# A node's own product in a graph layer: from additions on GpSimd during the sort to a trip through DRAM and additions on VectorE

## The chip, the cores and the metric

The kernel runs on one core of one Trainium2 chip. Its time is the device time of one execution in microseconds; the lower, the better. Of each kernel one execution is also recorded by the hardware profiler, and what is quoted as a view (the page, the timeline, the waits, the chain) is that one execution.

## What is computed

A network of two layers works on 6250 nodes of 256 float32 features. 100,000 edges (src, dst, weight) come sorted by dst. Layer 0's graph step sums over the edges towards their **src** node, so the edges have to be sorted anew; layer 1's sums towards their dst, in the order that is given.

```python
def _L0_gnn_ref(x, edge_row, edge_col, edge_val, weight_l, bias_l, weight_r, bias_r):
    h = x @ weight_l
    msgs = edge_val[:, None] * h[edge_col]
    agg = jax.ops.segment_sum(msgs, edge_row, num_segments=N)
    out = agg + bias_l
    out = out + x @ weight_r + bias_r        # x @ weight_r: the node's own product
    return out

x = x + _L0_gnn_ref(_layernorm(x), src, dst, edge_weight, ...)
x = x + _L0_ffn_ref(_layernorm(x), ...)      # 8 experts, softmax gates, three matmuls each
x = x + _L1_gnn_ref(_layernorm(x), src, dst, edge_weight, ...)
x = x + _L1_ffn_ref(_layernorm(x), ...)      # 32 experts, the best one for each node
```

## The kernel before, in words

The nodes stand in 49 tiles of 128, one node to a partition, and stay in SBUF for the whole kernel as `X` (128 x 49 x 256, float32). The work has three stages.

**The sort** (about the first 390 us) runs over 25 groups of 4096 edges. In each group VectorE builds one-hot patterns and ranks from them (`hot`, `same`, `picked`, `pos`), payloads (`loads`, line 527) and a one-hot of target places (`to`, line 523); TensorE counts (lines 464 to 474) and then moves the payloads to their places with 32 matmuls into `put` (line 530); ScalarE copies counts (`start`, `total`), multiplies the last payload (line 502) and takes the result out (`there`, line 533); GpSimd adds the pieces of the result into the table `Z` (lines 535 to 539) and notes sizes (line 489). `settle_group` updates running counts on VectorE in small instructions (lines 482, 484, 486, 488).

In between, each group also makes layer 0's products for two of the node tiles (`center0`, `products0`): the layer norm's statistics on VectorE (line 547), the centred rows on ScalarE (line 556), two transposes (line 340), four matmul passes that make both products at once (`ph`, line 570; the left half of the result is h, the right half the node's own product), and a copy with the factor of the norm into `hs` (line 571). GpSimd then adds the own product and the bias to `X` (lines 572 and 573), and SyncE's queue stores h in DRAM as `h0` (line 574).

**Layer 0** (about 390 to 1830 us). Its 15 blocks have 1, 1, 2, 3, then nine times 4, and 3 and 3 tiles. For a block, `edges0` reads the sorted edges out of `Z` on VectorE (lines 671 to 686) into an index list `idx`, of which three are kept. The generator `aggregate0` then goes over tiles and over 18 columns of 128 edges each: GpSimd gathers 128 rows of `h0` by an indirect DMA (line 201) into one of 12 buffers `g`, ScalarE and VectorE multiply by the edge weights (`m`, lines 230 and 231; six buffers), VectorE makes one-hots for three columns at a time (`s`, line 222), and TensorE accumulates in `acc` (line 701). After a tile's last column VectorE adds both halves of `acc` to `X` (line 704). The dense experts of an earlier block stand between these steps on TensorE (lines 748 and 760); how many columns come before each dense step is planned by `aheads`. VectorE adds each expert's result from PSUM to `X` (line 762). `end0` normalises the block and stores it as `h1` by SyncE's queue (lines 771 and 773). The first 64 columns of layer 1 already run here, with their own copies of indices and weights, `idx_e` and `w_e` (lines 806 to 812).

**Layer 1** (from about 1830 us) does the like with `h1`, in the edge order that is given.

Within an engine, instructions run in the order in which the built program has them. That order is made by a scheduler, which may move an instruction ahead of others of its engine where the data allow it; the diff alone doesn't show it.

Of the kernel before, what the change touches and what calls it, by code (L numbers as in the profile page):

```python
# [8 lines left out]
F32 = mybir.dt.float32  # L9
F32R = mybir.dt.float32r  # L10
BF = mybir.dt.bfloat16
I32 = mybir.dt.int32
AF = mybir.ActivationFunctionType
OP = mybir.AluOpType
AX = mybir.AxisListType

P = 128
N = 6250
D = 256
E = 100000  # L20
NT = 49
NLAST = N - (NT - 1) * P
NB = 4
EW = 18
# [25 lines left out]
def gnn_ffn_kernel(ctx: ExitStack, tc: tile.TileContext, a, out):  # L50
# [29 lines left out]

    nc = tc.nc

    const = ctx.enter_context(tc.tile_pool(name="const", bufs=1))
    dram = ctx.enter_context(tc.tile_pool(name="dram", bufs=1, space=bass.MemoryType.DRAM))
    work = ctx.enter_context(tc.tile_pool(name="work", bufs=2))

    X = const.tile([P, NT, D], F32, name="X")
    h0 = dram.tile([NT * P, D], F32, name="h0")  # L90
    h1 = dram.tile([NT * P, D], F32, name="h1")

    def across(name, pool=const):

        row = a[name]
        t = pool.tile([P, row.shape[0]], F32, name=name + "_b")
        nc.scalar.dma_start(t, bass.AP(tensor=row.tensor, offset=row.offset, ap=[[0, P], [1, row.shape[0]]]))
        return t
# [9 lines left out]
    src_c = const.tile([P, NCOL], I32, name="src_c")  # L108
    val_c = const.tile([P, NCOL], F32, name="val_c")
# [24 lines left out]
    early = sort_ctx.enter_context(tc.tile_pool(name="early", bufs=1))  # L134
    psum = sort_ctx.enter_context(tc.tile_pool(name="psum0", bufs=1, space=bass.MemoryType.PSUM))
# [51 lines left out]
    wlr = early.tile([P, 2, 2, D], F32, name="wlr")  # L187
    nc.scalar.dma_start(wlr[:, :, 0, :], a["L0_gnn_weight_l"].rearrange("(k p) d -> p k d", p=P))
    nc.scalar.dma_start(wlr[:, :, 1, :], a["L0_gnn_weight_r"].rearrange("(k p) d -> p k d", p=P))
    bias0 = across("L0_gnn_bias_l", early)  # L190
    bias0r = across("L0_gnn_bias_r", early)
    nc.gpsimd.tensor_add(bias0, bias0, bias0r)
    bias1 = across("L1_gnn_bias")
# [5 lines left out]
    def gather(pool, h, idx, ahead):  # L199
        g = pool.tile([P, D], F32, tag="g", name="g", bufs=ahead)  # L200
        nc.gpsimd.indirect_dma_start(out=g, out_offset=None, in_=h,  # L201
                                     in_offset=bass.IndirectOffsetOnAxis(ap=idx, axis=0))
        return g
# [14 lines left out]
    def one_hots(pool, dl, j, hots):  # L218

        s = pool.tile([P, SJ, P], F32R, tag="s", name="s", bufs=hots)  # L220
        n = min(SJ, dl.shape[1] - j)
        nc.vector.tensor_tensor(s[:, :n], col[:, None, :].to_broadcast([P, n, P]),  # L222
                                dl[:, j:j + n, None].to_broadcast([P, n, P]), OP.is_equal)
        return s

    def weighted(pool, h, idx, w, ahead, parts):

        g = gather(pool, h, idx, ahead)
        m = pool.tile([P, 2, D], F32R, tag="m", name="m", bufs=parts)
        nc.scalar.activation(m[:, 0, :], g, AF.Copy, scale=w)  # L230
        nc.vector.scalar_tensor_tensor(m[:, 1, :], g, w, m[:, 0, :], op0=OP.mult, op1=OP.subtract)  # L231
        return m
# [3 lines left out]
    def columns1(pool, psum, js, h, idx, w, bufs):  # L236


        hots, ahead, parts, few = bufs
        first = js.start == 0  # L240
        ends = []

        def summed(q, acc):

            yield
            if first and (q % 2 or q == 2 * NB):
                s = first_sums[:, q // 2, :]
            else:
                s = pool.tile([P, D], F32, tag="sums", name="sums", bufs=few)
            nc.scalar.activation(s, acc[:, 0, :], AF.Copy)  # L250
            nc.vector.tensor_add(s, s, acc[:, 1, :])
            halves[q] = s
            low, high = slice(0, P // 2), slice(P // 2, P)
            if q % 2:
                nc.vector.tensor_add(s[low], s[low], halves[q - 1][low])
            elif first:
                if 0 < q < 2 * NB:
                    nc.vector.tensor_add(halves[q - 1][high], halves[q - 1][high], s[high])
            else:
                if q == 2 * NB:  # L260
                    nc.vector.tensor_add(s, s, first_sums[:, NB, :])
                nc.vector.tensor_add(halves[q - 1][high], halves[q - 1][high], s[high])
                sT = pool.tile([P, 2, P], F32, tag="sT", name="sT", bufs=2)
                yield
                yield from by_weight(psum, halves[q - 1], sT, q // 2 - 1)

        for j in range(js.start, js.stop + (0 if first else LAG)):
            if j < js.stop:
                q, i = divmod(j + CS // 2, CS)
                opens = i == 0 or j == js.start  # L270
                done = i == CS - 1 or j == js.stop - 1
                if opens:
                    acc = psum.tile([P, 2, D], F32, tag="agg", name="acc", bufs=2)
                if (j - js.start) % SJ == 0:
                    s = one_hots(pool, dl_c, j, hots)
                m = weighted(pool, h, idx[:, j:j + 1], w[:, j:j + 1], ahead, parts)
                nc.tensor.matmul(acc, s[:, (j - js.start) % SJ, :], m, start=opens, stop=done)  # L277
                if done:
                    ends.append((j, summed(q, acc)))
            for at, steps in ends:  # L280
                if j - at in (0, 2, LAG - 4, LAG - 1):
                    next(steps, None)
            yield
        for _, steps in ends:
            for _ in steps:
                pass
        yield
# [271 lines left out]
    def products0(tiles, xn, std):  # L559

        n = len(tiles)
        rstd = work.tile([P, NB], F32, tag="rstd0", name="rstd0")
        nc.vector.reciprocal(rstd[:, :n], std[:, :n])
        hs = early.tile([P, 2, 2, D], F32, tag="hs", name="hs", bufs=2)
        for j, t in enumerate(tiles):
            nT = early.tile([P, 2, P], F32, tag="nT", name="nT", bufs=2)
            transposed(psum, xn[:, j, :], nT)
            ph = psum.tile([P, 2, D], F32, tag="mm", name="ph", bufs=2)
            for k in range(2):
                nc.tensor.matmul(ph, nT[:, k, :], wlr[:, k], start=(k == 0), stop=(k == 1))  # L570
            nc.scalar.activation(hs[:, j], ph, AF.Copy, scale=rstd[:, j:j + 1])
            nc.gpsimd.tensor_add(X[:, t, :], X[:, t, :], hs[:, j, 1, :])
            nc.gpsimd.tensor_add(X[:, t, :], X[:, t, :], bias0)
        nc.sync.dma_start(h0[tiles[0] * P:(tiles[0] + n) * P, :].rearrange("(t p) d -> p t d", p=P), hs[:, :n, 0, :])


    pairs = [[t for t in (2 * g, 2 * g + 1) if t < NT] for g in range(NG)]
# [41 lines left out]
    psum = dense_ctx.enter_context(tc.tile_pool(name="psum1", bufs=1, space=bass.MemoryType.PSUM))  # L619
# [12 lines left out]
    LIM = late[0] * P  # L632
    NE = EARLY * GC

    with tc.tile_pool(name="layer0", bufs=1) as wp, tc.tile_pool(name="outs0", bufs=1, side="right") as wo_pool, \
# [56 lines left out]
        def aggregate0():  # L692
            for b, tiles in enumerate(blocks0):
                idx, dl, w = edges[b]
                for i, t in enumerate(tiles):
                    acc = psum.tile([P, 2, D], F32, tag="agg", name="acc", bufs=2)
                    for j in range(EW):
                        if j % SJ == 0:
                            s = one_hots(wp, dl[:, i, :], j, 3)
                        m = weighted(wp, h0, idx[:, i, j:j + 1], w[:, i, j:j + 1], 12, 6)  # L700
                        nc.tensor.matmul(acc, s[:, j % SJ, :], m, start=(j == 0), stop=(j == EW - 1))  # L701
                        if j == EW - 1:
                            for half in range(2):
                                nc.vector.tensor_add(X[:, t, :], X[:, t, :], acc[:, half, :])
                        yield

            for _ in columns1(wp, psum, range(NE), h1[:LIM, :], idx_e, w_e, (3, 12, 6, 2)):
                yield
            while True:
                yield  # L710
# [84 lines left out]
        def load1(k, half):  # L795
# [4 lines left out]
            else:  # L800
                cs = slice(half * NC1 // 2, (half + 1) * NC1 // 2)
                x = a["L1_ffn_W2"].rearrange("e h d -> (e h) d").rearrange("(c p) d -> p c d", p=P)
                nc.sync.dma_start(w2f[:, cs, :], x[:, cs, :])


        idx_e = wp.tile([P, NE], I32, name="idx_e")
        w_e = wp.tile([P, NE], F32, name="w_e")

        def early_columns():
            nc.vector.tensor_scalar(w_e, src_c[:, :NE], float(LIM), None, op0=OP.is_lt)  # L810
            nc.vector.tensor_tensor(w_e, w_e, val_c[:, :NE], OP.mult)
            nc.vector.tensor_scalar(idx_e, src_c[:, :NE], float(LIM - 1), None, op0=OP.min)


        n_late = len(late)
# [67 lines left out]
        sums = Stream(aggregate0())  # L883
# [41 lines left out]
        hs = end0(late)  # L925
# [14 lines left out]
    with tc.tile_pool(name="layer1", bufs=1, reuse_waits="tile") as wp, \  # L940
# [74 lines left out]
        with tc.tile_pool(name="flow1", bufs=1, reuse_waits="tile") as flow:  # L1015

            sums = Stream(columns1(flow, psum, range(NE, NREAL), h1, src_c, val_c, (5, EW + 6, 12, 4)))
# [5 lines left out]
            for ins in done:  # L1023
                behind.enter_context(tc.issue_after(ins.ins))
            nc.vector.tensor_scalar(sel_x, which_x[:, :, None].to_broadcast([P, NX1, H1]), 0.0, FAR,
                                    op0=OP.is_equal, op1=OP.mult)
            nc.vector.memset(nought, 0.0)
            hm = hidden1(flow, block, 0)
            for b, tiles in enumerate(blocks1):
                n = len(tiles)  # L1030
# [79 lines left out]
```

## Time and profile before

| | us |
|---|---|
| three runs | 2892.92, 2898.83, 2900.43; median 2898.83 |
| the profiled execution | 2895.13, with a span of 2893.4 |
| TensorE busy in the span | 2677.7 (93%) |
| VectorE busy | 2012.4 (70%) |
| ScalarE busy | 1626.1 (56%) |
| GpSimd busy | 1926.1 (67%) |
| mean granted TensorE clock | 0.974 |

The span is the time from the first to the last recorded instruction; 1.7 us of the profiled execution lie around it. Busy shares are means over stages with different limits, so each stage has to be read by itself. GpSimd's gathers, x882 in layer 0, take 1.024 us each (line 201). GpSimd's additions of line 572 take 1.585 us in the mean and those of line 573 1.067 us, 48 of each within the first 375 us.

### The profile page before, as it was taken

Reading aid. Unit: us, or ns where it says so; the run is one execution under the profiler, and the core shown is the slowest. Engines: PE = TensorE matmul, PEld = TensorE weight load, DVE = VectorE, ACT = ScalarE, POOL = GpSimd, SP = SyncE. Lnnn points to the kernel's source line nnn. Section 1 sums busy time; section 2 is a strip of 40 time slices with the busy share of each in tenths; the row PEclk is TensorE's granted clock in tenths of the full one; section 3 lists DMA queues with packets and bytes.
Section 4 is the critical chain, followed back from the end, with each engine's and each line's share of the span. In section 5 each row is a group of like instructions: output and inputs, shape, how many; then the busy total and the mean of one; then the engine's idle time right before and its main releaser. Section 6 shows DMA issues by size and latency. Waiting matters only on the chain.

```text
span 2893.4 us, 37030 instructions
## 1 busy us (share of the span) xinstructions
PE 2677.7 (93%) x10336; PEld 1750.2 (60%) x10336; DVE 2012.4 (70%) x4917; ACT 1626.1 (56%) x3790; POOL 1926.1 (67%) x1932
## 2 busy tenths in 40 slices
PE   5888848888999999999999998779999999999998
PEld 2444427665566666666666665556666666666666
DVE  8999977778768767766566555666666666666630
ACT  6777737655555555555555545455555555555532
POOL 4666667777767676766675527677777777777720
PEclk9999978999999999999999999999999999999999
DMA  4000043333333333333332214333333333333310
GB/s 150 19 19 19 19 141 97 101 100 102 92 99 95 90 101 97 91 100 96 91 102 82 78 39 135 109 108 103 107 108 109 106 108 102 108 106 109 109 44 12
DMA packets 123140, 260.73 MB, mean 90 GB/s; under 512 B 32236, under 2 KB 68904, under 8 KB 122920
## 3 DMA queue, kind: packets, MB, share of 16 engines
q0 software_dynamic: 79872, 218.21, 26.2%
q1 hardware_dynamic: 31672, 32.42, 3.4%
q10 hardware_dynamic: 11376, 7.60, 0.8%
q8 instruction: 85, 1.39, 0.2%
q14 instruction: 135, 1.11, 0.1%
HBM read 238.87 MB, written 19.25 MB: 89 GB/s over the span
## 4 chain that ended last, share of the span: by engine, by line
PE 65%; DVE 17%; DMA 8%; issue 4%; ACT 4%; POOL 1%; ACTq 0%; POOLq 0%; DVEq 0%
PE ph L748 19%; PE py L760 10%; PE py L1000 9%; PE ph L984 9%; PE acc L701 6%; PE acc L277 4%; DMA g<-h,src_c 4%; DMA g<-h,idx 3%; DVE loads L527 3%; DVE to L523 2%; DVE m L231 2%; ACT m L230 2%; PE ph L987 1%; PE ph L214 1%; POOL g L201 1%
## 5 line engine op out<-in xcount | busy, mean ns | idle before, releaser
L201 POOL DMA_INDIRECT g<-h,idx x882 | 903.1, 1024 | 391.8 <-DVE m L231 175.2
L201 POOL DMA_INDIRECT g<-h,src_c x718 | 725.6, 1011 | 227.8 <-issue 104.2
L230 ACT ACTIVATE m<-g,w 128x256 fp32r<-128x256 f32 x882 | 394.7, 500 | 260.0 <-PE acc L701 136.0
L751 ACT ACTIVATE hT<-ph,shift,scale 128x512 f32<-128x512 f32 (+3 forms) x480 | 329.0, 696 | 314.6 <-PE ph L748 313.4
L230 ACT ACTIVATE m<-g,val_c 128x256 fp32r<-128x256 f32 x718 | 349.7, 503 | 273.6 <-PE acc L277 132.2
L231 DVE SCALAR_TENSOR_TENSOR m<-g,val_c,m 128x256 fp32r<-128x256 f32 x718 | 337.1, 483 | 211.2 <-ACT m L230 207.6
L231 DVE SCALAR_TENSOR_TENSOR m<-g,w,m 128x256 fp32r<-128x256 f32 x882 | 397.7, 476 | 42.5 <-ACT m L230 41.4
L748 PE MATMUL ph<-nT,w 128*128 128x512 f32 (+3 forms) x960 | 373.1, 524 | 25.0 <-ACT hT L751 24.8
L760 PE MATMUL py<-wo,hT 128*128 128x256 f32 x1568 | 382.1, 387 | 13.8 <-DVE X L762 10.5
L1000 PE MATMUL py<-w,hm 128*128 128x256 f32 x1568 | 386.7, 385 | 3.1 <-ACT hm L989 3.1
L701 PE MATMUL acc<-m,s 128*128 128x512 f32 x882 | 341.4, 490 | 38.0 <-DVE scale L657 24.7
L984 PE MATMUL ph<-nT,w 128*128 128x512 f32 (+2 forms) x832 | 374.8, 571 | 0.0
L748 PE MATMUL ph<-hT,w 128*128 128x512 f32 (+3 forms) x960 | 368.5, 518 | 0.5 <-ACT hT L751 0.5
L760 PEld LDWEIGHTS py<-wo,hT 128*128 128x128 f32 x1568 | 294.7, 193 | 80.8 <-DVE X L762 26.9
L277 PE MATMUL acc<-m,s 128*128 128x512 f32 x782 | 332.2, 499 | 1.7 <-DVE m L231 1.7
L1000 PEld LDWEIGHTS py<-w,hm 128*128 128x128 f32 x1568 | 292.1, 193 | 52.9 <-ACT hm L989 4.6
L222 DVE TENSOR_TENSOR s<-col,dl 128x384 fp32r<-128x384 f32 x294 | 161.4, 551 | 187.0 <-PE acc L701 184.8
L748 PEld LDWEIGHTS ph<-nT,w 128*128 128x128 f32 x960 | 175.2, 195 | 174.2 <-issue 118.1
L989 ACT ACTIVATE hm<-ph,b 128x512 f32<-128x512 f32 (+2 forms) x208 | 136.8, 659 | 200.0 <-PE ph L987 199.6
L748 PEld LDWEIGHTS ph<-hT,w 128*128 128x128 f32 x960 | 176.2, 193 | 118.9 <-issue 88.3
L701 PEld LDWEIGHTS acc<-m,s 128*128 128x128 f32 x882 | 169.7, 195 | 109.8 <-issue 48.9
L984 PEld LDWEIGHTS ph<-nT,w 128*128 128x128 f32 x832 | 157.2, 191 | 101.5 <-issue 81.1
(248 smaller groups left out, 3359.0 us busy)
## 6 DMA issues: line engine op xcount, KB each, us to landing
g<-h,idx POOLq DMA_INDIRECT x882, 2.8
g<-h,src_c POOLq DMA_INDIRECT x718, 2.8
h<-hs SPq DMA_DIRECT2D x25, 256.0 KB, 2.1
X<-in_x_dram SPq DMA_DIRECT2D x12, 512.0 KB, 8.9
out_dram<-o SPq DMA_DIRECT2D x11, 512.0 KB, 3.4
h<-hs SPq DMA_DIRECT2D x9, 512.0 KB, 3.0
w<-in_L_ffn_W_dram ACTq DMA_DIRECT2D x2, 2048.0 KB, 11.2
wo<-in_L_ffn_Wo_dram ACTq DMA_DIRECT2D x1, 2048.0 KB, 20.0
```

What stands on the lines that cost most here:

```text
L201: nc.gpsimd.indirect_dma_start(out=g, out_offset=None, in_=h, in_offset=bass.IndirectOffsetOnAxis(ap=idx, axis=0))
L222: nc.vector.tensor_tensor(s[:, :n], col[:, None, :].to_broadcast([P, n, P]), dl[:, j:j + n, None].to_broadcast([P, n, P]), OP.is_equal)
L230: nc.scalar.activation(m[:, 0, :], g, AF.Copy, scale=w)
L231: nc.vector.scalar_tensor_tensor(m[:, 1, :], g, w, m[:, 0, :], op0=OP.mult, op1=OP.subtract)
L277: nc.tensor.matmul(acc, s[:, (j - js.start) % SJ, :], m, start=opens, stop=done)
L701: nc.tensor.matmul(acc, s[:, j % SJ, :], m, start=(j == 0), stop=(j == EW - 1))
L748: nc.tensor.matmul(ph[:, :nw], (w1, w2)[layer][:, e, k, m * P:(m + 1) * P], src[:, k, :nw], start=(k == 0), stop=(k == 1))
L751: nc.scalar.activation(hT[:, m, :nw], ph[:, :nw], AF.Relu, bias=shift[:, layer, c:c + 1], scale=scale[:, layer, c:c + 1])
L760: nc.tensor.matmul(py, hT[:, k, j * P:(j + 1) * P], wo[:, e, k, :], start=(k == 0), stop=(k == 1))
L984: nc.tensor.matmul(ph[:, :nw], w1f[:, k, c * P:(c + 1) * P], nT[:, k, :nw], start=(k == 0), stop=False)
L989: nc.scalar.activation(hm[:, :nw], ph[:, :nw], AF.Relu, bias=b1[:, c:c + 1])
L1000: nc.tensor.matmul(py[:, j, :], now[:, cols], w2f[:, c, :], start=False, stop=(c == NC1 - 1), skip_group_check=True)
```

## The change

The sort no longer adds anything to `X`. `products0` stores both halves of `hs`: h in `h0`, as before, and the own product in a second DRAM tensor, `own0`. In layer 0, `aggregate0` loads the own product of each tile from `own0` into one of two buffers (`own`, by SyncE's queue) and lets VectorE add first the bias and then the own product to `X`; in the source these two additions stand before the tenth of a tile's 18 columns. The bias row stays in SBUF for the whole kernel, and for that and for the `own` buffers the gathers of layer 0 have 11 buffers instead of 12. The early columns of layer 1 use `src_c` and `val_c`, which are altered in place, and `idx_e` and `w_e` are gone, with one VectorE instruction fewer.

```diff
+    own0 = dram.tile([NT * P, D], F32, name="own0")
...
-    bias0 = across("L0_gnn_bias_l", early)
+    bias0 = across("L0_gnn_bias_l")
...
             nc.scalar.activation(hs[:, j], ph, AF.Copy, scale=rstd[:, j:j + 1])
-            nc.gpsimd.tensor_add(X[:, t, :], X[:, t, :], hs[:, j, 1, :])
-            nc.gpsimd.tensor_add(X[:, t, :], X[:, t, :], bias0)
-        nc.sync.dma_start(h0[tiles[0] * P:(tiles[0] + n) * P, :].rearrange("(t p) d -> p t d", p=P), hs[:, :n, 0, :])
+        for i, h in enumerate((h0, own0)):
+            nc.sync.dma_start(h[tiles[0] * P:(tiles[0] + n) * P, :].rearrange("(t p) d -> p t d", p=P), hs[:, :n, i, :])
...
                 for i, t in enumerate(tiles):
+                    own = wp.tile([P, D], F32, tag="sums", name="own", bufs=2)
+                    nc.sync.dma_start(own, own0[t * P:(t + 1) * P, :])
                     acc = psum.tile([P, 2, D], F32, tag="agg", name="acc", bufs=2)
                     for j in range(EW):
+                        if j == EW // 2:
+                            nc.vector.tensor_add(X[:, t, :], X[:, t, :], bias0)
+                            nc.vector.tensor_add(X[:, t, :], X[:, t, :], own)
                         if j % SJ == 0:
                             s = one_hots(wp, dl[:, i, :], j, 3)
-                        m = weighted(wp, h0, idx[:, i, j:j + 1], w[:, i, j:j + 1], 12, 6)
+                        m = weighted(wp, h0, idx[:, i, j:j + 1], w[:, i, j:j + 1], 11, 6)
...
-            for _ in columns1(wp, psum, range(NE), h1[:LIM, :], idx_e, w_e, (3, 12, 6, 2)):
+            for _ in columns1(wp, psum, range(NE), h1[:LIM, :], src_c, val_c, (3, 11, 6, 2)):
...
-        idx_e = wp.tile([P, NE], I32, name="idx_e")
-        w_e = wp.tile([P, NE], F32, name="w_e")
         def early_columns():
-            nc.vector.tensor_scalar(w_e, src_c[:, :NE], float(LIM), None, op0=OP.is_lt)
-            nc.vector.tensor_tensor(w_e, w_e, val_c[:, :NE], OP.mult)
-            nc.vector.tensor_scalar(idx_e, src_c[:, :NE], float(LIM - 1), None, op0=OP.min)
+            nc.vector.scalar_tensor_tensor(val_c[:, :NE], src_c[:, :NE], float(LIM), val_c[:, :NE],
+                                           op0=OP.is_lt, op1=OP.mult)
+            nc.vector.tensor_scalar(src_c[:, :NE], src_c[:, :NE], float(LIM - 1), None, op0=OP.min)
```

## The prediction, made before the changed kernel was run

> **What bounds the kernel now.** I read the busy time of the engines by stretches first, since the page's shares are means over stages. Columns: stretch, its length, then PE, PEld, DVE, ACT and POOL busy (instructions), granted clock, DMA share, GB/s.
>
> ```profile
> 200.00:250.00 50.00, 43.60 (x199) 22.43 (x198) 49.98 (x109) 38.19 (x142) 30.94 (x34) 1.00 0.05 17
> ...
> 500.00:600.00 100.00, 82.23 (x358) 67.12 (x358) 72.78 (x181) 62.87 (x137) 77.00 (x75) 0.91 0.37 101
> ...
> 800.00:1000.00 200.00, 199.82 (x692) 126.03 (x692) 146.37 (x368) 113.70 (x216) 139.83 (x139) 1.00 0.34 97
> ```
>
> Three limits. In the sort VectorE never rests (49.98 of 50). From 800 us to about 1700 TensorE never rests. Between them GpSimd issues gathers without a break: 75 in 100 us at 1.03 us each, with 0.30 us between two, which leaves nothing of the 100. That ramp is paced by the gathers.
>
> Next, VectorE's timeline in the sort: start, duration, line. The first four rows are a usual group (at 254 us), the last four come from groups where no addition on GpSimd lay beside the instruction.
>
> ```profile
> 254.11 0.75 DVE L482 SCALAR_TENSOR_TENSOR ZJ<-base_of,part,full_of 128x49 bf16<-128x49 bf16 x1
> ...
> 254.75 0.73 DVE L484 TENSOR_SCALAR wrap<-total 128x49 f32<-128x49 f32 x1
> ...
> 255.58 0.67 DVE L486 TENSOR_TENSOR base_of<-total,wrap 128x49 bf16<-128x49 f32 x1
> ...
> 257.13 0.88 DVE L497 TENSOR_TENSOR same<-tq 128x256 bf16<-128x256 bf16 x1
> ...
> 35.09 0.20 DVE L486 TENSOR_TENSOR base_of<-total,wrap 128x49 bf16<-128x49 f32 x1
> ...
> 36.16 0.40 DVE L497 TENSOR_TENSOR same<-tq 128x256 bf16<-128x256 bf16 x1
> ...
> 46.89 0.40 DVE L482 SCALAR_TENSOR_TENSOR ZJ<-base_of,part,full_of 128x49 bf16<-128x49 bf16 x1
> ...
> 47.72 0.18 DVE L484 TENSOR_SCALAR wrap<-total 128x49 f32<-128x49 f32 x1
> ```
>
> Four small instructions take 0.75 + 0.73 + 0.67 + 0.88 = 3.03 us where 1.18 would do. GpSimd's timeline has its four additions exactly there:
>
> ```profile
> 251.99 2.63 POOL L572 TENSOR_TENSOR X<-X,hs 128x256 f32<-128x256 f32 x1 [0.53 <-ACT hs L571]
> 254.70 0.73 POOL L573 TENSOR_TENSOR X<-X,L_gnn_bias_l_b 128x256 f32<-128x256 f32 x1
> 255.39 0.79 POOL L572 TENSOR_TENSOR X<-X,hs 128x256 f32<-128x256 f32 x1
> 256.26 1.47 POOL L573 TENSOR_TENSOR X<-X,L_gnn_bias_l_b 128x256 f32<-128x256 f32 x1
> ```
>
> So VectorE loses 1.85 us in each group of 14.30 to them. That looks like 40 us over the sort. The decisive question is who waits for VectorE. The start of `put` on TensorE, with the idle time before it in brackets:
>
> ```profile
> 96.92 0.84 PE L530 MATMUL put<-loads,to 128*128 128x245 bf16 x3
> ...
> 111.18 0.83 PE L530 MATMUL put<-loads,to 128*128 128x245 bf16 x3
> ...
> 125.42 0.84 PE L530 MATMUL put<-loads,to 128*128 128x245 bf16 x3
> ...
> 381.61 7.40 PE L530 MATMUL put<-loads,to 128*128 128x245 bf16 x32 [3.04 <-DVE to L523]
> ```
>
> While VectorE still had some lead, TensorE went round in 14.26 and 14.24 us. Its loop has its own waits, all on ScalarE after TensorE's own results (0.88 us for `start`, 0.88 for `nT`, seen in every group). VectorE goes round in 14.30. Freed of 1.85 us, VectorE would be ready early and TensorE's loop would bind at 14.24.
>
> [...]of the gathers of layer 1, the 165 that lie beside VectorE's additions of two SBUF tiles exceed the shortest (0.94) by 0.087 us in the mean, and so do the others. [...]line 776, the same kind, took 411 here, and 0.34 from one start to the next. [...]the store of `h0` landed in 2.1.
>
> **The change part by part.**
>
> *98 additions leave GpSimd.* First group: `over` (0.73 against 0.18 to 0.27) and `to` (2.52 against 2.27) stand beside line 572 and 573, and `put` waits 2.71 us for `to`: 0.75 us gained. Fourth group: `put` waits 0.70 for a `to` of 2.75: 0.70. From 139.66 to 368.42, 16 rounds in 228.76 us, 14.297 each; 14.24 instead: 0.9. Last group: `put` waits 3.04, VectorE being behind; it would be up to 4.5 us ahead, held back only by `total`: 3.0. Sum **-5.4 us**. The rest of the 40 us becomes idle time of VectorE.
>
> *25 more stores of 256 KB on SyncE's queue.* DMA is 5 to 7% busy there, `hs` has two buffers of 28 us; the load for `check_edges` stands one store later, needed 15 us after. Nothing.
>
> *The start of layer 0.* The built program's order moves the additions far forward: on VectorE six bias and six own additions stand before the first `m`. 12 x 0.34 = 4.1 us; but the small work of `missing` and `early_columns`, and about 2.4 us of a later block's `edges0`, leave the same place. I count the first `m` 0.6 us earlier, and the first index list 0.15 earlier. The first own load is issued when the sort has ended, and its addition comes some 2.8 us later: against 2.1 us of landing it may wait, 0 to 1 us; I take +0.3.
>
> *The ramp, up to gather 270 (770 us).* 19 own and 19 bias additions fall there, 13 us of VectorE. They are hidden: VectorE itself stands still for 8.2 us at the end of the ramp, because a new `idx` has to wait for gather 270, eight gathers beyond its own `m`:
>
> ```profile
> 770.05 0.20 DVE L682 TENSOR_SCALAR idx<-bothi 128x72 int32<-128x72 int32 x1 [8.24 <-DMA g<-h,idx]
> ...
> 772.82 3.78 PE L760 MATMUL py<-wo,hT 128*128 128x256 f32 x8 [3.88 <-DVE X L762]
> ```
>
> In the new order it stands at the same `m`, so the pace stays the gathers'. If each addition holds up a gather by 0 to 0.14 us, that costs 0 to 5; from the 165 gathers I take 0.03: +1.2. Eleven buffers suffice: the lead of gathers over `m` I count in the ramp is at most about 7, and in the 8 us stop the queue gets just 11 ahead.
>
> *The stretch that TensorE binds.* The remaining 24 own and 24 bias additions (16 us) crowd in the next 110 us or so. Cover: line 222 waits 30.1 us for TensorE between 760 and 1000. But own loads have two buffers, so each starts when the addition two before is done and lands 2.1 us or more later; in places three stand close together, and VectorE then waits, some 5 us in all, with evictions (line 762) behind it. I take +0.8, 0 to 4. SyncE's stores of `h1` stand behind own loads whose buffers are by then free; nobody waits for them. After it, layer 0's tail and layer 1 are as before: nothing.
>
> Sum: -5.4 + 0.3 + 1.2 + 0.8 = **-3.1 us** on the profiled 2895.1, whose span is 2893.4. The median of the runs is 3.7 above that execution, so: 2898.8 - 3.1 = 2895.7.
>
> **The rivals.**
> *VectorE's relief passes on* (faster). If TensorE's loop shortens with VectorE, because ScalarE's order was waiting for it after all, 22 groups x 1.85 = 41 us: 2858; a third of it gives 2885. For it: VectorE is 100% busy and the chain of waits runs through it. Against: TensorE's rounds of 14.24 with VectorE ahead, and ScalarE's idle 2.9 us per group, all on `put`.
> *The own loads stall VectorE* (slower). 18 of them come while the count of `m` stands between 307 and 334. Two buffers and 2.1 us make about 19 us of waiting, plus 13 us of additions, in a stretch of some 38 us; TensorE's evictions have two PSUM buffers. It decides when waits and additions there exceed what line 222 waits anyway; with half uncovered, +15 - 3 = 2911.
> *The change isn't what the source says*: that holds already, since the additions run ahead of their columns instead of in the midst; it only moves costs between ramp and later stretch.
>
> **How the numbers follow.** A difference under 0.3% (8.7 us) is about what a measurement of this kernel can tell from no change. The likeliest case, 0.6, has its own range 2890 to 2901. The faster rival, with orders of the new program that happen to fit better, 0.24; the slower one 0.16. Within the likeliest a few hundredths pass the bound on the fast side. Faster 0.3, same 0.53, slower 0.17. The range reaches from a fifth of the faster rival to two thirds of the slower: 2882 to 2908.
>
> **What would show it.** Right: lines 482, 484, 486, 497 back near 1.2 us together, VectorE with idle time in the sort, `put` every 14.24 us, its last wait gone, the stage's end some 5 us earlier; gathers still back to back to about 765; TensorE full from 800 to 1700. Wrong: rounds of `put` well under 14.2, long waits on `own` loads on VectorE with TensorE idle behind, or gathers above 1.1 us.

## The result, and the profile after

The changed kernel takes **2911.85 us** (median of six runs, 2905.60 to 2916.97) against 2898.81 of the kernel before in the same session: a ratio of 1.0045, 95% interval 1.0030 to 1.0061. It is slower by 13 us; the prediction had 3 us faster, with 2908 as its upper end. The profiled execution took 2907.63, with a span of 2905.8 (before: 2893.4).

On the chips of the first seven experiments (no_adds, no_load, eleven, pinned, no_adds_again, adds_in_sort, late_in_sort) the kernel before took 3229 to 3282 us. There the product that reads a gather started late: in no_adds 10.3 us after the gather's end (median of the first 264), where it was 2.8 in the kernel before. Why is not known. So of these seven I read the sort and the durations of instructions, and their ratios carry little.

In the changed kernel, lines 482 to 571 of the sort stand two lower (484 to 573), and line 201 is now 203, 231 is 233, 682 is 683, 701 is 708, 762 is 769. First the busy time by stretches, with the columns of the same view before (length; PE, PEld, DVE, ACT, POOL; clock, DMA share, GB/s):

```profile
200.00:250.00 50.00, 42.92 (x191) 22.11 (x190) 45.33 (x114) 40.64 (x152) 23.15 (x24) 1.00 0.10 32
500.00:600.00 100.00, 78.25 (x342) 61.36 (x343) 70.36 (x184) 61.85 (x134) 77.61 (x74) 0.95 0.37 101
800.00:1000.00 200.00, 196.87 (x679) 123.32 (x678) 161.76 (x420) 111.40 (x211) 143.44 (x134) 0.99 0.37 106
```

VectorE now rests in the sort: 45.33 busy of 50, where it was 49.98. The additions turn up in the last row: VectorE 161.76 where it was 146.37, and TensorE, which never rested, lacks 3 us.

VectorE's timeline of the changed kernel in a usual group of the sort, the same four instructions as before:

```profile
263.18 0.40 DVE L484 SCALAR_TENSOR_TENSOR ZJ<-base_of,part,full_of 128x49 bf16<-128x49 bf16 x1
...
263.57 0.28 DVE L486 TENSOR_SCALAR wrap<-total 128x49 f32<-128x49 f32 x1
...
263.95 0.21 DVE L488 TENSOR_TENSOR base_of<-total,wrap 128x49 bf16<-128x49 f32 x1
...
266.67 0.41 DVE L499 TENSOR_TENSOR same<-tq 128x256 bf16<-128x256 bf16 x1
```

They take 1.30 us together instead of 3.03. TensorE's timeline at `put`:

```profile
108.07 7.37 PE L532 MATMUL put<-loads,to 128*128 128x245 bf16 x32
...
122.26 7.37 PE L532 MATMUL put<-loads,to 128*128 128x245 bf16 x32
...
363.59 7.37 PE L532 MATMUL put<-loads,to 128*128 128x245 bf16 x32
...
375.44 7.39 PE L532 MATMUL put<-loads,to 128*128 128x245 bf16 x32 [1.71 <-DVE to L525]
```

A round takes 14.19 us, and the last `put` starts at 375.44 instead of 381.61. So the sort gained what was forecast, and what follows it lost three times as much. Where, is read from the gathers. The row of the page, before and then after (count; busy, mean ns of one; idle before them, with the releaser of most of it):

```profile
L201 POOL DMA_INDIRECT g<-h,idx x882 | 903.1, 1024 | 391.8 <-DVE m L231 175.2
```

```profile
L203 POOL DMA_INDIRECT g<-h,idx x882 | 920.3, 1043 | 391.7 <-DVE m L233 167.0
```

GpSimd doesn't wait more, its gathers are longer. How that looks is seen at the start of layer 0, in the timeline of the changed kernel (the rows of VectorE and GpSimd alone):

```profile
395.61 0.41 DVE L704 TENSOR_TENSOR X<-X,own 128x256 f32<-128x256 f32 x1
395.88 2.30 POOL L203 DMA_INDIRECT g<-h,idx  x1 [0.30 <-issue]
395.94 1.08 DVE L676 TENSOR_TENSOR there<-at,Z 128x900 f32<-128x900 bf16 x1
396.95 0.41 DVE L703 TENSOR_TENSOR X<-X,L_gnn_bias_l_b 128x256 f32<-128x256 f32 x1
397.29 1.08 DVE L678 TENSOR_REDUCE both<-there 128x36 f32<-128x900 f32 x1
398.29 0.41 DVE L704 TENSOR_TENSOR X<-X,own 128x256 f32<-128x256 f32 x1
398.49 2.06 POOL L203 DMA_INDIRECT g<-h,idx  x1 [0.30 <-issue]
398.62 1.08 DVE L676 TENSOR_TENSOR there<-at,Z 128x900 f32<-128x900 bf16 x1
```

Where VectorE's instructions of lines 676, 703 and 704 stand close together here, the two gathers beside them took 2.30 and 2.06 us; the median of layer 0's gathers is 0.95. Line 676 stood in the kernel before as well; lines 703 and 704 are the additions that were moved.

The loss, stage by stage, in the two profiled executions (after minus before): the last `put` -6.2 us and the first gather -6.3; gather 264 +2.1. Between the two, the gathers' busy time grew by 8.3 (280.8 to 289.1) and the gaps between them stayed at 80 us. Then come two stops. VectorE's and TensorE's timeline of the changed kernel there:

```profile
771.96 0.20 DVE L683 TENSOR_SCALAR idx<-bothi 128x72 int32<-128x72 int32 x1 [8.98 <-DMA g<-h,idx]
775.72 0.79 PE L708 MATMUL acc<-m,s 128*128 128x512 f32 x1 [7.79 <-DVE m L233]
...
884.31 0.20 DVE L683 TENSOR_SCALAR idx<-bothi 128x72 int32<-128x72 int32 x1 [5.25 <-DMA g<-h,idx]
887.72 3.60 PE L767 MATMUL py<-wo,hT 128*128 128x256 f32 x8 [2.78 <-DVE X L769]
```

At both, VectorE waits for the gather that frees an index list. TensorE's gap at the first grew from 3.88 to 7.79 us, and a second gap of 2.78 is new. The order of VectorE's instructions has a part in it: from the end of the first stop to the next `m` it took 3.2 us, and 1.5 in the kernel before. In the stretch from 690 to 890 TensorE lacks 11.5 us of work instead of 5.5. After 940 the changed kernel stays 9 to 10 us behind until layer 1, read at each block's normalisation.

### The profile page after: what moved, and what is told of

Its sections match the earlier page's. It is cut to its first block, busy times and chain, and to the rows that moved or that the text cites. A ratio compares the mean times of both kernels' runs of the same rounds, so it can differ in the third digit from the quotient of the medians.

```text
span 2905.8 us, 37090 instructions
## 1 busy us (share of the span) xinstructions
PE 2684.4 (92%) x10276; PEld 1751.4 (60%) x10336; DVE 2004.4 (69%) x5014; ACT 1624.9 (56%) x3790; POOL 1854.6 (64%) x1834
## 4 chain that ended last, share of the span: by engine, by line
PE 63%; DMA 8%; DVE 8%; issue 4%; ACT 3%; POOL 1%; ACTq 0%; POOLq 0%; DVEq 0%
PE ph L755 19%; PE py L767 9%; PE py L1004 9%; PE ph L988 9%; PE acc L708 5%; PE acc L279 5%; DMA g<-h,src_c 4%; DMA g<-h,idx 3%; DVE m L233 2%; ACT m L232 1%; POOL g L203 1%; PE ph L216 1%; PE tr L342 1%; PE ph L991 1%; PE pl L727 1%
## 5 line engine op out<-in xcount | busy, mean ns | idle before, releaser
L203 POOL DMA_INDIRECT g<-h,idx x882 | 920.3, 1043 | 391.7 <-DVE m L233 167.0
L203 POOL DMA_INDIRECT g<-h,src_c x782 | 791.4, 1012 | 297.0 <-issue 114.2
L232 ACT ACTIVATE m<-g,val_c 128x256 fp32r<-128x256 f32 x782 | 379.6, 503 | 301.2 <-PE acc L279 144.0
L233 DVE SCALAR_TENSOR_TENSOR m<-g,val_c,m 128x256 fp32r<-128x256 f32 x782 | 366.3, 483 | 219.1 <-ACT m L232 214.6
```

## The experiments

The ratios are to the kernel before in the same session. The table has what counts in each profile, which is one execution: the additions that VectorE makes in layer 0, and how many start before gather 276; the busy time of the first 276 gathers; how many of the 882 gathers lie beside an addition (0.15 us of overlap or more), with their mean, and the mean of the others; how much TensorE lacks between 690 and 890 us. A long gather is likelier to lie beside an addition than a short one, so the mean of those beside overstates what an addition costs. Single executions scatter: "after" and no_load_timed have the same additions and differ by 5 us in what TensorE lacks.

| kernel | additions | by gather 276 | 276 gathers, us | beside, mean us | others, us | TensorE lacks, us | ratio (95%) |
|---|---|---|---|---|---|---|---|
| before | 0 | 0 | 292.9 | - | 1.024 | 5.5 | 1 |
| after | 98 | 51 | 302.4 | 52: 1.49 | 1.016 | 11.5 | 1.0045 (1.0030-1.0061) |
| no_adds_timed | 0 | 0 | 294.2 | - | 1.036 | 6.1 | 0.9985 (0.9977-0.9992) |
| no_load_timed | 98 | 51 | 304.5 | 52: 1.46 | 1.025 | 16.9 | 1.0036 (1.0024-1.0049) |
| stt_form | 98 | 51 | 308.1 | 54: 1.54 | 1.029 | 15.4 | 1.0075 (1.0052-1.0097) |
| double | 196 | 85 | 305.7 | 83: 1.59 | 1.017 | 17.9 | 1.0114 (1.0079-1.0150) |
| halves | 196 half | 85 | 299.8 | 100: 1.17 | 1.030 | 13.6 | 1.0080 (1.0048-1.0111) |
| pinned_timed | 98 | 30 | 294.0 | 75: 1.29 | 1.018 | 8.6 | 1.0014 (1.0005-1.0023) |
| mixed | 66 | 0 | 294.9 | 53: 1.34 | 1.034 | 6.6 | 1.0010 (1.0003-1.0017) |
| idx_four | 98 | 54 | 301.6 | 57: 1.46 | 1.021 | 7.9 | 1.0012 (1.0002-1.0022) |
| before_idx_four | 0 | 0 | 290.7 | - | 1.038 | 2.0 | 0.9964 (0.9950-0.9977) |
| mixed_idx_four | 66 | 0 | 297.6 | 54: 1.33 | 1.045 | 1.9 | 0.9962 (0.9951-0.9973) |

### Is it the additions, the loads or the buffers?

**no_adds, no_adds_again, no_adds_timed** are one kernel, run three times:

```diff
-                    own = wp.tile([P, D], F32, tag="sums", name="own", bufs=2)
-                    nc.sync.dma_start(own, own0[t * P:(t + 1) * P, :])
...
-                        if j == EW // 2:
-                            nc.vector.tensor_add(X[:, t, :], X[:, t, :], bias0)
-                            nc.vector.tensor_add(X[:, t, :], X[:, t, :], own)
```

> The changed kernel without the own loads and without the two additions in layer 0; the own products are still stored. It leaves out the own product and the bias of layer 0. Its TensorE order is exactly the one of the kernel before, its GpSimd order the one of the changed kernel. Theory A (the 98 additions on VectorE, with the order that they bring, cost layer 0 its time; the sort's gain is real): 6 us below the kernel before, about 2893, 19 below the changed kernel. Theory B (the eleventh buffer or the 25 stores cost it, the additions are hidden): within 3 us of the changed kernel, 2909 to 2912, with the sort still 6 us shorter.

> The kernel of no_adds once more (no own loads, no additions; own product and bias of layer 0 are left out), since in the first four runs every kernel's gathers landed late and all times lay near 3280. Theory A (VectorE's additions and the order that comes with them cost layer 0 its time): 6 us below the kernel before, ratio 0.998, about 2893. Theory B (the eleventh buffer or the stores): ratio 1.003 to 1.0045.

> The kernel of no_adds (changed kernel without own loads and additions in layer 0; own product and bias of layer 0 left out). Theory A (the additions and the order they bring make the loss): 2890 to 2894, ratio 0.997 to 0.999, gathers of layer 0 at 900 to 907 us. Theory B (buffers, stores): 2905 or more.

no_adds gave 0.9985 (0.9960 to 1.0010), no_adds_again 0.9957 (0.9933 to 0.9980), with 899 and 907 us of gathers in layer 0. The third, where the time can be read, gave 2897.17 against 2902.39. Its last `put` starts at 374.5. So without the additions the changed kernel is, by the ratio, 4.4 us faster than the kernel before, and with them 13 slower: the additions and the order that comes with them cost some 17 us, and neither the stores nor the eleventh buffer made the loss. Within one session, no_load_timed below took 2913.02, 16 us more than no_adds_timed. The gathers of layer 0 took 913.5 us here, more than expected; their sum over the whole layer varies by up to 14 us between executions of this one kernel, and the sum of the first 276 (290.7 to 294.2 in the three timed kernels without additions) is the steadier measure. By it, 51 additions cost the gathers much the same in three pairs, each from another session: 9.5 us from before to after, 10.3 from no_adds_timed to no_load_timed, 11.1 from no_adds to no_load.

**no_load, no_load_timed**: no own loads, the bias added twice.

```diff
-                    own = wp.tile([P, D], F32, tag="sums", name="own", bufs=2)
-                    nc.sync.dma_start(own, own0[t * P:(t + 1) * P, :])
...
-                            nc.vector.tensor_add(X[:, t, :], X[:, t, :], own)
+                            nc.vector.tensor_add(X[:, t, :], X[:, t, :], bias0)
```

> The changed kernel without the own loads: the second addition adds the bias row again, so the own product is left out (and the bias comes twice); VectorE has the same number of additions. Theory A (VectorE's additions themselves): within 3 us of the changed kernel, 2909 to 2913. Theory C (the slower rival of the prediction: VectorE waits for own loads that two buffers hold up): 10 us or more below the changed kernel, 2902 or less. The changed kernel's trace shows one such wait of 2.3 us only, which speaks for A.

> The kernel of no_load (no own loads, the second addition adds the bias again; the own product is left out). Theory A: within 3 us of the changed kernel, 2909 to 2914. Theory C (waits for own loads): 2902 or less.

no_load gave 0.9980 (0.9958 to 1.0001), no_load_timed 2913.02, ratio 1.0036. The loss stays without any load: theory C, the prediction's slower rival, falls. The changed kernel's waits of VectorE between 760 and 1000 say the same (total, times, longest; in us):

```profile
DVE idx L683 <- DMA g<-h,idx: 18.3, 3, 9.0
DVE s L224 <- PE acc L708: 15.1, 4, 5.5
DVE X L769 <- PE py L767: 5.6, 9, 1.3
DVE X L704 <- DMA own<-own: 2.3, 1, 2.3
```

One wait of 2.3 us for an own load in all, instead of the rival's 19.

**eleven**: the kernel before with 11 buffers.

```diff
-                        m = weighted(wp, h0, idx[:, i, j:j + 1], w[:, i, j:j + 1], 12, 6)
+                        m = weighted(wp, h0, idx[:, i, j:j + 1], w[:, i, j:j + 1], 11, 6)
...
-            for _ in columns1(wp, psum, range(NE), h1[:LIM, :], idx_e, w_e, (3, 12, 6, 2)):
+            for _ in columns1(wp, psum, range(NE), h1[:LIM, :], idx_e, w_e, (3, 11, 6, 2)):
```

> The kernel before with 11 buffers for the gathers in place of 12, in layer 0 and in the early columns. Theory A: no difference, 2898 to 2900. Theory B (the buffer is what costs): 5 us or more above the kernel before, 2904 or more, with gathers that wait longer for m between 560 and 800 us.

0.9988 (0.9965 to 1.0011): too wide to tell by itself. no_adds_timed, with 11 buffers and below the kernel before, excludes it as the cause.

### How much does an addition cost, and does its form matter?

**double** does each addition twice, **halves** splits each into two of 64 partitions, **stt_form** writes it as another instruction.

```diff
-                            nc.vector.tensor_add(X[:, t, :], X[:, t, :], own)
+                            for _ in range(2): nc.vector.tensor_add(X[:, t, :], X[:, t, :], own)      # double
+                            nc.vector.tensor_add(X[q, t, :], X[q, t, :], own[q])                      # halves, q = each half
+                            nc.vector.scalar_tensor_tensor(X[:, t, :], X[:, t, :], 1.0, own, op0=OP.mult, op1=OP.add)   # stt_form
```

(the bias likewise)

> The changed kernel with each of the two additions of a tile done twice (the own product and the bias of layer 0 count twice in the output), 196 full additions in place of 98. Theory G: twice the excess, gathers of layer 0 at 936 to 942 us. Theory J (the longer gathers come from the loads of own or the changed order, and not from the additions): 918 to 924.

> The changed kernel with each addition of layer 0 split in two of 64 partitions, as the additions of layer 1 are that the prediction was calibrated on: 196 instead of 98, twice VectorE's time. Theory G, with the number of partitions as what made layer 1's additions cheap: gathers of layer 0 at 904 to 912 us in all. Theory I (64 partitions hold GpSimd up as long as 128, and layer 1's additions were cheap for another reason): 930 to 940.

> The changed kernel with its 98 additions of layer 0 written as scalar_tensor_tensor (X times 1.0 plus the other operand); TensorE's and VectorE's orders stay the same. What counts is the busy time of the 882 gathers of layer 0 on GpSimd: 904 us in the kernel before, 921 in the changed one, 900 and 907 without the additions, so that each addition seems to hold the gathers up by 0.18 us. Theory G ([...]the form of the instruction decides how much): 905 to 913, since the scalar_tensor_tensor of line 233 costs the gathers beside it some 0.2 to 0.3 us per us and the additions some 0.5 to 0.6. Theory H (the place counts, not the form: any VectorE instruction of that length costs as much there): 918 to 925.

The page's row of the gathers, in double, then halves, then stt_form:

```profile
L203 POOL DMA_INDIRECT g<-h,idx x882 | 944.2, 1071 | 388.9 <-DVE m L233 170.9
```

```profile
L203 POOL DMA_INDIRECT g<-h,idx x882 | 922.3, 1046 | 401.5 <-DVE m L233 185.4
```

```profile
L203 POOL DMA_INDIRECT g<-h,idx x882 | 935.0, 1060 | 385.0 <-DVE m L233 163.1
```

Twice the additions gave 944 us of gathers and 2930.78 us: theory J falls. How large the excess is depends on what it is counted from. The kernels without additions had 903.1 us in the first session and 913.5 and 915.4 in later ones, so it is 29 to 41 us in double and 7 to 19 in halves. Over the first 276 gathers, against the 290.7 to 294.2 without additions, 85 full additions cost 11 to 15 us, 85 on 64 partitions 6 to 9, and 51 in the other form 14 to 17. So an addition on 64 partitions held the gathers up about half as much as a full one (0.07 to 0.11 us against 0.13 to 0.18), for about the same time on VectorE (in the changed kernel layer 1's additions of 64x256 took 0.42 us, those of 128x256 0.41); 922 is neither G's nor I's number. The form brings no relief at all (935): in this point theory G's expectation falls and H's number is exceeded.

That layer 1's additions, on which the prediction was calibrated, have 64 partitions is only a part of why they looked harmless. In halves the gathers beside an addition were 0.14 us longer than the others (1.17 against 1.03), in layer 1 of the kernel before some 0.02. What made up the rest is not shown.

In double and halves the scheduler also gave TensorE another order: of some 4900 matmuls between 400 and 1850 us, some 4500 stand in the same sequence, while in stt_form all do. Each of the two ran only twice. So their times show that more additions cost more, but not by which way.

### Does the place matter?

**pinned, pinned_timed** hold a tile's additions behind the `m` of its ninth column:

```diff
                         if j == EW // 2:
-                            nc.vector.tensor_add(X[:, t, :], X[:, t, :], bias0)
-                            nc.vector.tensor_add(X[:, t, :], X[:, t, :], own)
+                            with tc.issue_after(last_ms[-1].ins):
+                                nc.vector.tensor_add(X[:, t, :], X[:, t, :], bias0)
+                                nc.vector.tensor_add(X[:, t, :], X[:, t, :], own)
```

> The changed kernel with each tile's two additions held behind the m of the tile's ninth column in VectorE's order, where the source has them, so that the scheduler can't put them earlier; all 49 tiles then have their additions spread over the layer instead of before gather 335. Theory D (it is the crowding between 700 and 940 us, which the scheduler made, that costs): most of the 19 us between the sort's gain and the changed kernel goes, 2894 to 2900. Theory A in its narrow form (each addition costs wherever it stands): 2908 to 2912.

> The kernel of pinned (each tile's two additions held behind the m of its ninth column). Theory D (the crowding of 98 additions before gather 335 makes the loss): after 770 us TensorE binds and the gathers have slack, so only the 16 tiles of the ramp still cost, about 32 additions of 0.18 us: 2896 to 2901. Theory A in its narrow form (each addition costs wherever it stands): 2908 to 2912.

pinned gave 0.9975 (0.9957 to 0.9993). pinned_timed: 2906.39, ratio 1.0014, by the ratios some 9 us better than the changed kernel (7 better than no_load_timed in the same session) and 8 us short of no_adds_timed. No addition stands before the first `m` (12 did), and 30 instead of 51 start by gather 276. These gathers are back at 294.0 us here; in pinned, with the same 30 additions, they took 297.3 where no_adds took 288.4, so it is not settled that spreading spares the gathers. Of the stops one is left, in the timeline of pinned_timed (VectorE's stop, then TensorE's gap):

```profile
765.22 0.20 DVE L685 TENSOR_SCALAR idx<-bothi 128x72 int32<-128x72 int32 x1 [6.94 <-DMA g<-h,idx]
```

```profile
771.10 3.78 PE L770 MATMUL py<-wo,hT 128*128 128x256 f32 x8 [6.98 <-DVE X L772]
```

So by the times the crowding made about half of the loss (theory D in part); spread additions still cost.

**mixed** leaves tiles 0 to 15 to GpSimd in the sort; the other 33 go through DRAM and are pinned.

```diff
+            if t < EASY:                                   # EASY = 16
+                nc.gpsimd.tensor_add(X[:, t, :], X[:, t, :], hs[:, j, 1, :])
+                nc.gpsimd.tensor_add(X[:, t, :], X[:, t, :], bias0)
...
-                        if j == EW // 2:
+                        if t >= EASY and j == EW // 2:
```

> Tiles 0 to 15: own product and bias added by GpSimd in the sort, as in the kernel before. Tiles 16 to 48: through DRAM and added by VectorE, held behind the m of the tile's ninth column, as in pinned. The sort keeps GpSimd's additions in its first 8 groups only. Theory A with the ramp as the place (an addition costs only where the gathers pace the work): the ramp as before, the sort's end 4 to 7 us earlier, 2892 to 2896 on a kernel before of 2898.8, ratio 0.9975 to 0.999. If additions cost in the later stretch as well (33 tiles, 12 us of gathers): ratio 1.001 or more.

2906.84, ratio 1.0010. The sort's end comes at 376.6, 5 us earlier than before, but the gain is gone by the end. At the block of 826 us mixed is still 3.6 us ahead of the kernel before, at 1456 it is 2.1 behind. TensorE's timeline of mixed shows a gap in each of six blocks from 877 to 1407 us, at the stop for `idx` (two of them, with the wait):

```profile
877.49 1.99 PE L774 MATMUL py<-wo,hT 128*128 128x256 f32 x8 [0.78 <-DVE X L776]
...
983.35 1.99 PE L774 MATMUL py<-wo,hT 128*128 128x256 f32 x8 [0.79 <-DVE X L776]
```

They add up to 5.3 us. VectorE stands still at these stops for 4.2 to 5.5 us; in the kernel before it did so for 3.2 to 3.5, and TensorE had no gap there. So the expectation that an addition is free where TensorE binds was wrong, at least while that stop is there; in mixed_idx_four below, without the stop, nothing more is lost after the block of 826 us than in before_idx_four.

### Is the stop for an index list the cause?

**idx_four**, **before_idx_four** and **mixed_idx_four** have four lists instead of three (and before_idx_four 11 gather buffers, to make room):

```diff
-            idx = wp.tile([P, NB, EW], I32, tag="idx", name="idx", bufs=3)
+            idx = wp.tile([P, NB, EW], I32, tag="idx", name="idx", bufs=4)
```

> The changed kernel with four index lists idx instead of three, all else the same. The additions still lengthen the gathers (915 us or more in layer 0). Theory K (late gathers become time where VectorE stands still for the gather that frees an idx, 9.0 and 5.3 us, with TensorE idle 7.8 and 2.8 us behind it): these stops go, TensorE is idle less than 2 us between 760 and 900, 6 to 12 us below the changed kernel, 2900 to 2906. Theory L (the gathers pace the ramp, a stop merely shows their lag): the wait moves to m, at most 3 us below, 2908 to 2912.

> The kernel before with four index lists idx and, to make room, 11 buffers for the gathers. Theory K (the stop at idx turns late gathers into time; before, the gathers are late by less): TensorE's one gap of 3.9 us at 770 us goes, 2 to 5 us below the kernel before, ratio 0.998 to 0.9995. If the fourth list helps both kernels alike, 8 us or more below, ratio 0.997 or less, and idx_four says nothing of this change.

> The kernel of mixed with four index lists. If the gain of the sort and that of the fourth list add up: ratio 0.9965 to 0.998. If the stop at idx was only the place where a lag became visible: as mixed.

idx_four: 2907.04, ratio 1.0012. By the ratios that is 10 us better than the changed kernel, within theory K's 6 to 12. But before_idx_four gains as much, 2892.98 against 2904.13, which by its own expectation means that idx_four says nothing of this change. With four lists the two kernels differ by 1.0012 / 0.9964 = 1.0048, with three by 1.0045. In the stretch 690 to 890 TensorE lacks 2.0 and 7.9 us with four lists, 5.5 and 11.5 with three: 6 us of difference in both, though each is one execution and such numbers scatter by as much as 5 us. Where the gaps go when the stop is gone is seen in TensorE's timeline of idx_four:

```profile
782.38 0.51 PE L708 MATMUL acc<-m,s 128*128 128x512 f32 x1 [1.26 <-DVE m L233]
...
852.62 1.13 PE L767 MATMUL py<-wo,hT 128*128 128x256 f32 x4 [1.81 <-DVE X L769]
868.21 0.49 PE L708 MATMUL acc<-m,s 128*128 128x512 f32 x1 [2.61 <-DVE m L233]
```

By the ratios, theory K falls: the stop is a cost of its own, in both kernels, and the additions' lag shows elsewhere once it is gone. before_idx_four beats both kernels. mixed_idx_four (2894.11, 0.9962) adds nothing to it that could be measured, although its last `put` starts 5.4 us earlier.

### Could the additions stay in the sort, on VectorE?

**adds_in_sort**: both lines 572 and 573 on VectorE. **late_in_sort**: the same, one group later and held behind `to`.

```diff
-            nc.gpsimd.tensor_add(X[:, t, :], X[:, t, :], hs[:, j, 1, :])
-            nc.gpsimd.tensor_add(X[:, t, :], X[:, t, :], bias0)
+            nc.vector.tensor_add(X[:, t, :], X[:, t, :], hs[:, j, 1, :])      # adds_in_sort
+            nc.vector.tensor_add(X[:, t, :], X[:, t, :], bias0)
...
+        with tc.issue_after(tos[-1].ins):                                     # late_in_sort
+            for t, own in some:                                               # the group before
+                nc.vector.tensor_add(X[:, t, :], X[:, t, :], own)
+                nc.vector.tensor_add(X[:, t, :], X[:, t, :], bias0)
```

> The kernel before with both additions of a node tile in the sort, as before, but on VectorE instead of GpSimd; no trip through DRAM, 12 buffers. VectorE gets back 1.85 us in each group and takes up 4 x 0.34 = 1.36 us. If TensorE's loop binds as soon as VectorE is free of GpSimd: the sort ends 4 to 6 us earlier and layer 0 is as before, ratio 0.998, 2893. Rival: the additions wait for hs, which ScalarE makes late in a group, and hold up the next group's one-hots on VectorE: the sort is 1 us or more longer in each of 24 groups, ratio 1.008 or more.

> The kernel before with the additions in the sort on VectorE, as in adds_in_sort, but one group later and each behind the line to of its group, so that no hs can be late. VectorE is freed of 1.85 us per group and takes up 4 x 0.34 = 1.36 us. Theory E (what made adds_in_sort 47 us longer in the sort is VectorE waiting for hs, 1.7 to 3.1 us each time): rounds of put back to 14.2 to 14.3 us, the last put at 375 to 380 us, 2 to 6 us below the kernel before in all, ratio 0.998 to 0.999. Rival F (the order of the matmuls of ph and the transposes, which the scheduler changed in both kernels, made the rounds longer): rounds of 15 us or more again, ratio 1.008 or more.

adds_in_sort: ratio 1.0166 (1.0116 to 1.0216); the last `put` starts at 428.8. VectorE's timeline, two groups in a row:

```profile
264.08 0.43 DVE L572 TENSOR_TENSOR X<-X,hs 128x256 f32<-128x256 f32 x1 [1.70 <-ACT hs L571]
...
278.08 0.43 DVE L572 TENSOR_TENSOR X<-X,hs 128x256 f32<-128x256 f32 x1 [3.06 <-ACT hs L571]
```

VectorE waits for `hs` with the next `loads` and `to` behind it, and the rounds alternate between 14.8 and 17.8 us: the rival named there, and larger than expected. late_in_sort: 1.0007 (0.9985 to 1.0030). The rounds are 14.4 us in the mean (13.8 and 14.9 in turn) and the last `put` starts at 381.9, as in the kernel before. VectorE no longer waits for `hs`, so theory E holds in the cause and F falls, but its 2 to 6 us didn't come: the four additions take up about what VectorE was freed of.

## Why the prediction was wrong

In the two profiled executions the parts were: -6.2 us up to the last `put`, +8.3 from the first gather to gather 264, +7.1 from there to the block of 931 us, +3.2 after it; 12.4 together, where -3.1 was forecast. (Read as sizes, the range's lower end, 2882, is two fifths of the faster rival's 41 us and not a fifth.)

**The sort, -5.4: right.** The last `put` came 6.2 us earlier, with rounds of 14.19 where 14.24 was forecast, and a wait of 1.71 left at the last. That the sum fits is in part luck: the last group gave 1.3 where 3.0 was forecast, and about 2 us lie in the second round, where nothing was. That round took 20.0 us in the kernel before's profile and 18.0 in eleven, with the same additions; against eleven the gain is 4.2. VectorE's relief was not passed on: that rival is refuted, as its counter-argument said.

**The start of layer 0, +0.3: too small.** The first gather and the first `m` came as forecast (0.1 and 0.5 us earlier, measured from the last `put`), and no own load was waited for there. But gathers 0 to 11 took 16.3 us instead of 13.8, beside the twelve additions.

**The ramp, +1.2: the step that failed.** It was 38 additions at 0.03 us of gather each, from the gathers of layer 1 that lie beside additions of two SBUF tiles. Up to gather 264 the gathers in fact grew by 8.3 us (2.5 of them at the start), with some 50 additions by then: 0.17 each, above even the 0.14 that was taken as the upper end. The calibration rested on the wrong instructions. Layer 1's additions have 64 partitions, those that were moved have 128, and halves shows that this matters (0.07 to 0.11 us each against 0.13 to 0.18). Counted again, some 80 to 110 gathers of layer 1 lie beside such an addition, depending on the overlap that is asked for, and not 165; they exceed the shortest by 0.08 to 0.09 us, the others by 0.07. Line 776 of the kernel before, the same 128x256 addition, could not have told: only eight gathers lie beside it. But line 675 could, which multiplies two tiles of SBUF on 128 partitions. The kernel before's timeline (the rows of line 675 and of GpSimd alone):

```profile
453.48 0.95 POOL L201 DMA_INDIRECT g<-h,idx  x1 [0.30 <-DVE m L231]
...
454.63 1.10 DVE L675 TENSOR_TENSOR there<-at,Z 128x900 f32<-128x900 bf16 x1
454.73 1.82 POOL L201 DMA_INDIRECT g<-h,idx  x1 [0.30 <-DVE idx L682]
```

The 75 gathers of layer 0 that lie beside it took 1.31 us in the mean, the others 1.00: 23 us of gathers for 54 us of line 675. At that rate an addition of 0.41 us costs 0.18, an estimate close to the 0.17 that came. That an addition leaves the gathers beside it nearly as they are was the author's estimate; for one of 128 partitions no trace had shown it. Measured, 51 additions lengthened 276 gathers by 9.5 to 11.1 us. Which part of a gather is held up, no run tells.

**"They are hidden", by VectorE's stop for `idx`: wrong in kind.** The stop waits for gather 270. Later gathers move its end, so it is no cover against a cost that falls on the gathers. The stop stayed (8.24 to 8.98), and behind it stand a reduction, `at`, a bias addition and another instruction of `edges0` before the next `m`, so TensorE's gap doubled to 7.79.

**The stretch that TensorE binds, +0.8: the mechanism was wrong.** No waits for own loads, but a second stop with a gap of 2.78; the changed kernel fell back by a further 5 us between the blocks' normalisations at 826 and 931. How much of this is the gathers, how much VectorE's added time and how much the new order of VectorE and TensorE, is open. Eleven buffers did suffice in the ramp (no gap between gathers grew); at the stop one gather waited 3.5 us for a buffer.

**"The own loads stall VectorE", 2911:** the right number for a reason that no_load_timed refutes. "Nothing" for the rest is not refuted: layer 1 took 2 us longer in the profile of after, but in the ten kernels timed in later sessions, with and without the change, it took 4 to 8 us longer than in the profile of before.

**Open** remains why so little of the sort's 5 us reaches the end where the ramp has no additions: in mixed_idx_four the first 276 gathers took 6.9 us more than in before_idx_four. How the gathers happen to fall on VectorE's dense stretches could do it; no run tells. It is open likewise how much of the loss is VectorE's own 33 us and how much is the gathers' growth: every experiment changed both. halves hints that VectorE's time counts, since its gathers grew no more than the changed kernel's and it was slower (1.0080), but with two executions and another order it doesn't prove it. And no kernel has the changed kernel's order of TensorE and VectorE without its additions, so the order's own share isn't known either.

## What to carry to other kernels

Work that moves to VectorE beside a stream of gathers can cost twice, in VectorE's time (here 98 additions of 0.34 us, 33 in all) and in the gathers' length (9.5 to 11.1 us for the first 51 of them); calibrate the second on an instruction with as many partitions (85 additions cost the first 276 gathers 6 to 9 us on 64, 11 to 15 on 128) that does lie beside gathers, as line 675 did, not on the nearest name. A stop that ends with the very stream that you lengthen is no slack (here 8.24 us became 8.98): ask what ends it before you hide work under it. And an engine that is 100% busy while another one's loop binds gives back little when it is freed: here 1.85 us per group on VectorE became 0.1 per round.

## What was not expected of the hardware

Additions of two 128x256 float32 tiles on VectorE (0.34 us from one start to the next) lengthened the gathers that GpSimd issues beside them: 51 of them made 276 gathers 9.5 to 11.1 us longer in three pairs of kernels, 0.2 us for each addition. Writing the addition as scalar_tensor_tensor didn't help (308.1 us for these gathers, 302.4 with the plain form), and splitting it by partitions about halved the excess per instruction (for the same 276 gathers, 85 halves 6 to 9 us, 85 full additions 11 to 15), not per tile.
